# Keeping eleven instead of ten of sixteen key tiles of an attention in SBUF, with the closing layer norm redistributed over the engines

## The chip, the core and the metric

The kernel runs on one core of one Trainium2 chip, as one program. The metric is the device time of one execution in microseconds (us). Before the change it is 3533.81 us, the median of three runs (3532.12 to 3534.32). An engine's name is short: PE is the matrix engine (TensorE), DVE the vector engine, ACT the scalar engine, POOL is GpSimd, SP the engine that issues the DMAs.

## The reference

Two layers act on `x` (2 batches, 2048 tokens, 512 features), both modulated by a vector `cond` for each batch. The first is a state-space block (S5) with a feed-forward part. The change touches nothing of it. The second is the attention:

```python
def _sln(h, w, ln_g, ln_b, Wg, bg, Wb, bb):
    mu = jnp.mean(h, axis=-1, keepdims=True)
    var = jnp.mean((h - mu) ** 2, axis=-1, keepdims=True)
    ln = (h - mu) / jnp.sqrt(var + EPS) * ln_g + ln_b
    return (w @ Wg.T + bg)[:, None, :] * ln + (w @ Wb.T + bb)[:, None, :]
...
    h = _sln(hidden, w, ln_g, ln_b, Wg, bg, Wb, bb)
    qkv = (h @ Wqkv.T + bqkv).reshape(B, N, num_heads, hd, 3)
...
    energy = jnp.einsum('bhqd,bhkd->bhqk', q, k)
    att = jax.nn.softmax(energy, axis=-1) / D ** 0.5
    out = jnp.einsum('bhqk,bhkd->bhqd', att, v)
...
    out = out @ Wp.T + bp
    h1 = out + hidden
    h2 = _sln(h1, w, ln_g, ln_b, Wg, bg, Wb, bb)
    return h2 + h1
```

There are 16 heads of 32 features. The softmax goes over 2048 keys, and its maximum is taken exactly, for each query.

## The kernel before

**Up to about 1400 us** the S5 and feed-forward layers run. They leave `x2` (the residual), the keys `kd`, the queries `qd` and the values `vd` in DRAM.

**The attention** fills the rest. It is cut into 64 *blocks*: one block is one pair of heads against one chunk of 512 queries of one batch. Batch 0 has blocks 0 to 31, batch 1 (called `LB`) blocks 32 to 63. A block has 16 key tiles of 128 keys. It is worked in 8 *periods* of 2 key tiles. Periods are numbered through by `j`. `j % 8` is called the *phase* here: phase 0 is the first period of a block. The loop over `j` writes the order of every engine by hand; nothing reorders it.

For a key tile, the scores `s` (128 keys by 2 heads by 512 queries) are made on PE in PSUM (`raw_scores`, two banks, double-buffered). To subtract the maximum before the exponential, the maximum over all keys must be known first. The kernel does this in two ways:

- `NX` = 10 tiles of a block are *kept*. `AHEAD` = 15 periods before their use, `keep` makes their scores, ACT copies them into a tile of the `ring` (21 SBUF tiles, L766), and DVE folds them into a running maximum `run` (L771; the first tile of a block, tile 0, needs no fold of its own).
- The other 6 are made twice: first, ahead, in `across` with queries and keys exchanged (`m`, 384 key columns for each of 2 products, L780), from which DVE takes a maximum along the row (L785); and again at their use in `make` (L755), where DVE adds the negative maximum while it moves them out of PSUM (L820).

`turn_run` transposes the running maximum (PE, four 128x128, twice a block) and reduces it on DVE (L792). `spread` transposes the result (`pt_neg`, L802), has ACT copy it, and sends it through DRAM back to all partitions as `shift`. `take_off` adds `shift` to a kept tile on POOL (L814), in place. `exponentials` is ACT (L825). `weighted` multiplies by the values one period later (PE, 8 instructions, L835).

So a period is, in the order of PE: anything due, then either one `make` and `across` and one `keep`, or `across` and two `keep`s, and last the eight `o` products. Two `keep`s at once stand in phases 0 and 4. In those phases both tiles that are used are kept ones, so no `make` is needed. `twice` = (3, 7) names these periods counted in the block that is read ahead.

PSUM has 8 banks: `s` two times two, `m` two, one called `pt` and one for `o`. `m` and `pt` have one buffer each. `pt` is shared by the transposes of `turn_run` and `spread`, by the output projection `py` of batch 0 and by `z` of the closing norm. Two instructions of different engines that read the same bank are put in order by semaphores: the fold of a kept tile on DVE waits until ACT has copied it.

**The output** of a batch is finished per row tile of 128 queries: `fetch` loads, `divide` divides by the softmax sums (POOL), `project` multiplies by `wp` (PE, 8 instructions of 512 columns, L906), `residual`, `statistics`, `newton` (reciprocal square root, on ACT as one chain of 128x1 instructions), `last_norm` (ACT, into `z` in PSUM), `gain` (DVE), `close` (POOL and the store). For batch 0 its 16 row tiles run beside blocks 34 to 59, two for every three blocks, with one group of `project` in a period. For batch 1 twelve row tiles run from block 60 on, one every two periods. The last four are finished by `end_last`, after the last block. `after(j, ...)` puts work at the start of period `j`, `closing(j, ...)` behind that period's keeps and exponentials.

Of the kernel before, what the change touches and what calls it, by code (L numbers as in the profile page):

```python
# [19 lines left out]
P = 128  # L20
# [19 lines left out]
def tile_s5_block_then_sln_attention(  # L40
# [49 lines left out]
    one_half = const.tile([P, 1], F32, name="one_half")  # L90
    nc.gpsimd.memset(one_half, 1.5)
# [609 lines left out]
    NX = 10  # L701
# [4 lines left out]
    ring = ctx.enter_context(tc.tile_pool(name="ring", bufs=21, side="right"))  # L706
# [169 lines left out]
    def fetch(b, qt):  # L876

        at = slice(qt * P, (qt + 1) * P)
        o4 = work.tile([P, NG, P], F32, name="o4")
        nc.sync.dma_start(o4, od[b][:, at].rearrange("(g r) q -> r g q", r=P))  # L880
        by = work.tile([P, NG, P], F32, name="by")
        heads = invd[b][:, at].rearrange("(g j) q -> j g q", j=4)
        for j in range(4):
            nc.sync.dma_start(
                by[32 * j : 32 * j + 32, :, :], heads[j : j + 1, :, :].to_broadcast([32, NG, P])
            )
        xr = work.tile([P, D], F32, name="xr", bufs=4)
        nc.sync.dma_start(xr, x2[b][at, :])
        held[b, qt] = o4, by, xr
# [19 lines left out]
    def residual(b, qt):  # L909

        o4, h, py = held[b, qt]
        nc.vector.tensor_add(h, py, h)
        held[b, qt] = h

    def statistics(b, qt):

        h = held[b, qt]
        st = small.tile([P, 6], F32, name="st3")
        nc.vector.bn_stats(st, h)
        mv = small.tile([P, 2], F32, name="mv3")  # L920
        nc.vector.bn_aggr(mv, st)
        v = small.tile([P, 1], F32, name="v3")
        y = small.tile([P, 1], F32, name="scale3", bufs=4)
        shift = small.tile([P, 1], F32, name="shift3", bufs=4)
# [5 lines left out]
        nc.vector.tensor_scalar(shift, mv[:, 0:1], -1.0, None, ALU.mult)  # L930
        held[b, qt] = h, y, shift, v

    def newton(b, qt, turns, final):

        h, y, shift, v = held[b, qt]
        for _ in range(turns):
            c = small.tile([P, 1], F32, name="c3")
            nc.scalar.activation(c, y, AF.Identity, scale=y)
            nc.scalar.activation(c, c, AF.Identity, bias=one_half, scale=v)
            nc.scalar.activation(y, c, AF.Identity, scale=y)  # L940
        if final:
            nc.scalar.activation(shift, shift, AF.Identity, scale=y)

    def last_norm(b, qt):

        h, scale, shift, _ = held[b, qt]
        z = ps.tile([P, CH], F32, name="z", tag="pt")
        nc.scalar.activation(z, h, AF.Identity, bias=shift, scale=scale)
        held[b, qt] = h, z

    def gain(b, qt):

        h, z = held[b, qt]
        nc.vector.tensor_tensor(z, z, ending[b][0], ALU.mult)
        nc.vector.tensor_tensor(h, z, h, ALU.add)

    def close(b, qt):

        h, z = held.pop((b, qt))
        nc.gpsimd.tensor_tensor(h, h, ending[b][1], ALU.add)  # L960
        nc.sync.dma_start(out[b, qt * P : (qt + 1) * P, :], h)
# [9 lines left out]
    def end_fetch():  # L971
# [12 lines left out]
        late = P - 2 * HD  # L984
        nc.gpsimd.memset(ends["o"][1][late:, 1, :], 0.0)
        nc.gpsimd.memset(ends["w"], 0.0)
        nc.gpsimd.tensor_copy(ends["turn"], ident)
        for e in range(2):
            to, of = 3 * HD * e, HD + HD * e
            nc.sync.dma_start(ends["w"][to : to + HD, :], wp[late + HD * e : late + HD * e + HD, NG - 1, :])  # L990
            nc.gpsimd.tensor_copy(ends["turn"][:, to : to + HD], ident[:, of : of + HD])

    def end_fetch_more():
        cols = slice(LC * CH, (LC + 1) * CH)
        nc.sync.dma_start(ends["o"][1][: P // 2, 1, :], od[LB][D - P : D - P // 2, cols])

    def end_divisors(heads):
        cols = slice(LC * CH, (LC + 1) * CH)
        for j in heads:
            at = slice(HD * (j % 4), HD * (j % 4) + HD)  # L1000
# [4 lines left out]
    def end_divide(g, rows=P):  # L1005
        o, by = ends["o"][g // 2][:rows, g % 2, :], ends["by"][g // 2][:rows, g % 2, :]
        nc.gpsimd.tensor_tensor(o, o, by, ALU.mult)
# [19 lines left out]
    def end_last(o):  # L1027
        raw, inv, on = (spare(n)[:, 0, :] for n in ("raw4", "inv4", "on4"))
# [7 lines left out]
        for i, at in enumerate(parts):  # L1036
            nc.vector.reciprocal(inv[:, at], turned[:, i, :])
            nc.vector.tensor_tensor(on[:, at], o[:, at], inv[:, at], ALU.mult)
        end_project(1, list(range(NG - 1)))
        for i in range(2):  # L1040
            end_project(i, [NG - 1])
        mv = small.tile([P, TT, 2], F32, name="mv4")
        hts = [spare("ht01"), spare("ht23")]
        g_row, t_row = ending[LB]
        for i in range(2):
# [8 lines left out]
            nc.scalar.copy(hts[i], ends["py", i])  # L1054
        v = small.tile([P, TT], F32, name="v4")
        scale = small.tile([P, TT], F32, name="scale4")
        shift = small.tile([P, TT], F32, name="shift4")
        nc.vector.tensor_scalar(v, mv[:, :, 1], EPS, None, ALU.add)
        rsqrt(v, scale, TT)
        nc.vector.scalar_tensor_tensor(shift, mv[:, :, 0], -1.0, scale, ALU.mult, ALU.mult)  # L1060
        for t in range(TT):
            z = ends["py", t // 2][:, t % 2, :]
            nc.scalar.activation(
                z, z, AF.Identity, bias=shift[:, t : t + 1], scale=scale[:, t : t + 1]
            )
        for t in range(TT):
            qt = LC * TT + t
            y, z = hts[t // 2][:, t % 2, :], ends["py", t // 2][:, t % 2, :]
            nc.vector.tensor_tensor(z, z, g_row, ALU.mult)
            nc.vector.tensor_tensor(y, z, y, ALU.add)  # L1070
            (nc.gpsimd if t < TT - 1 else nc.vector).tensor_tensor(y, y, t_row, ALU.add)
            nc.sync.dma_start(out[LB, qt * P : (qt + 1) * P, :], y)
# [5 lines left out]
    AHEAD = 15  # L1078
    NP = 8
    twice = (3, 7)  # L1080
# [28 lines left out]
    SPREAD = -3  # L1109
    OPEN = -4  # L1110
    for i, n in enumerate(opens):
        free = NP * (max(m for m in range(N) if pair_of[m] == i - 2) + 1) if i > 1 else FIRST
        after(max(free if i > 1 else FIRST, NP * n - AHEAD - 11), load_k, i)
        after(max(OPEN + 2, NP * n - 9), load_v, i)
    for n in range(N):
        after(max(FIRST + 1 + n, NP * n - AHEAD - 6), load_q, n)
        after(NP * n - AHEAD + NP + 1, turn_run, n, 0)
        after(NP * n - AHEAD + NP + 3, turn_run, n, 1)
        after(NP * n + SPREAD, spread, n)
    for b in range(NB):  # L1120
        for c in range(NQ):
            j = NP * (blocks.index((b, NPAIR - 1, c)) + 1) + 1
            if (b, c) == (LB, LC):
# [8 lines left out]
                after(j + 5, end_divisors, range(NH - 4, NH - 2))  # L1132
                for g in range(NG - 1):
                    after(j + 3 + g, end_divide, g)
                after(j + 8, end_divide, NG - 1, P // 2)
# [8 lines left out]
            for t in range(TT):  # L1144
                qt = c * TT + t
                if b == LB:
# [6 lines left out]
                    closing(k + 3, newton, b, qt, 2, False)  # L1153
                    closing(k + 4, newton, b, qt, 1, True)
                    closing(k + 4, last_norm, b, qt)

                    (after if (k + 5 - SPREAD) % NP == 0 else closing)(k + 5, gain, b, qt)
                    closing(k + 6, close, b, qt)
                else:

                    k = NP * (NPAIR * NQ * (b + 1) + 2 + 3 * qt // 2) + 3
                    after(k - 2, fetch, b, qt)
                    after(k + 2, divide, b, qt)
                    for g in range(NG):
                        after(k + 3 + g, project, b, qt, (g,))
                    closing(k + 6, residual, b, qt)
                    closing(k + 7, statistics, b, qt)
                    for i in range(3):
                        closing(k + 8 + i, newton, b, qt, 1, i == 2)

                    k += 2 if t % 2 else 8
                    closing(k + 10, last_norm, b, qt)
                    closing(k + 11, gain, b, qt)
                    after(k + 13, close, b, qt)
# [120 lines left out]
```

## Time and profile before

The profiled execution took 3533.44 us; its span in the trace is 3531.7 us, with 34142 instructions.

| | PE | DVE | ACT | POOL |
|---|---|---|---|---|
| busy, us | 3378.7 | 2204.6 | 1976.7 | 1943.5 |
| share of the span | 96% | 62% | 56% | 55% |

The start times of the 64 `pt_neg` transposes, one for each block, three periods before it begins, give the length of a block:

| blocks | what runs beside | length of one block, us |
|---|---|---|
| 2 to 33 | nothing | 28.8 |
| 35 to 58 | norm and projection of batch 0 | 32.6, 33.2, 32.3 in turn |
| 61, 62 | norm and projection of batch 1 | 51.7, 52.7 |
| from the last `pt_neg` to the end | the last five periods, `end_last` | 96.0 |

How it is read: a busy PE counts a matmul from issue to its modelled end, so pipelined matmuls overlap, and busy PE time isn't PE at its peak. Start-to-start distances are what it sustains. The granted clock of PE is full nearly everywhere; six short stretches after 1400 us are at half clock, where PE had just stood idle.

### The profile page before, as it was taken

The page shows a single profiled execution, that of the slowest core. Times are in us where ns is not written, and L with a number is a line of the kernel's source. Part 1 is how long each engine was busy: PE and PEld are TensorE (multiplying, and loading weights), DVE is VectorE, ACT ScalarE, POOL GpSimd, SP SyncE. Part 2 cuts the span into 40 slices and gives each one's busy share as a digit, 9 for nine tenths or more (in the row PEclk, how much of TensorE's full clock was granted, in tenths as well). Part 3 has the DMA queues.
Part 4 walks back from the last instruction along what each step waited for, and adds up shares of the span by engine and source line. Part 5 has one row for each costly group of instructions (what it writes and reads, how often), then busy time and mean ns, then how long its engine had stood idle before and what let it go on. Part 6 is the DMA issues. An engine that isn't in the chain of part 4 may idle for free.

```text
span 3531.7 us, 34142 instructions
## 1 busy us (share of the span) xinstructions
PE 3378.7 (96%) x11772; PEld 1534.2 (43%) x11772; DVE 2204.6 (62%) x2937; ACT 1976.7 (56%) x2430; POOL 1943.5 (55%) x982
## 2 busy tenths in 40 slices
PE   7999999999999999899999999999999999999977
PEld 4444444444444444444444444444444444444432
DVE  6233232323232212689999999998888888888864
ACT  2111111111111111488888888888888888888865
POOL 4223131313131311288877888888687787777764
PEclk8999999999999999999999999999999999999999
DMA  8001111111111012332213222222233333323222
GB/s 298 1 30 42 48 39 45 39 50 37 48 36 42 33 45 74 99 71 65 71 50 73 71 65 65 53 72 66 68 85 84 81 76 79 88 71 80 61 89 93
DMA packets 201542, 236.92 MB, mean 67 GB/s; under 512 B 89755, under 2 KB 118939, under 8 KB 197273
## 3 DMA queue, kind: packets, MB, share of 16 engines
q1 hardware_dynamic: 201368, 234.74, 23.9%
q8 instruction: 93, 1.52, 0.2%
q14 instruction: 81, 0.66, 0.1%
HBM read 166.77 MB, written 67.76 MB: 66 GB/s over the span
## 4 chain that ended last, share of the span: by engine, by line
PE 71%; DVE 14%; ACT 11%; issue 2%; DMA 1%; POOL 1%; SPq 0%; DVEq 0%; ACTq 0%; POOLq 0%
PE o L835 14%; PE ph L489 13%; PE po L502 12%; PE s L755 9%; DVE run L771 8%; PE pk L532 6%; ACT x L766 4%; PE pv L544 3%; PE py L906 3%; ACT x L825 3%; PE m L780 2%; ACT pT L825 2%; DVE pT L820 2%; PE pt_run L791 2%; PE pu L423 2%
## 5 line engine op out<-in xcount | busy, mean ns | idle before, releaser
L814 POOL TENSOR_TENSOR x<-x,shift 128x1024 f32<-128x1024 f32 x640 | 1502.7, 2388 | 343.4 <-DMA shift<-flat 269.4
L766 ACT COPY x<-s 128x1024 f32<-128x1024 f32 x640 | 633.7, 1011 | 234.0 <-PE s L755 232.3
L755 PE MATMUL s<-qs,ks 128*128 128x512 f32 x2048 | 703.1, 433 | 51.7 <-DVE run L771 46.8
L825 ACT ACTIVATE x<-x 128x1024 f32<-128x1024 f32 x640 | 675.9, 1057 | 6.7 <-POOL x L814 6.6
L771 DVE TENSOR_TENSOR run<-s,run 128x1024 f32<-128x1024 f32 x512 | 625.4, 1221 | 82.1 <-ACT x L766 64.4
L835 PE MATMUL o<-x,v 128*64 128x512 f32 x2560 | 664.2, 614 | 2.0 <-ACT raw L844 2.0
L820 DVE TENSOR_TENSOR pT<-s,shift 128x1024 f32<-128x1024 f32 x384 | 467.6, 1218 | 55.0 <-PE s L755 50.4
L785 DVE TENSOR_REDUCE top<-m 128x1 f32<-128x768 f32 x512 | 485.8, 949 | 25.7 <-PE m L780 25.4
L755 PEld LDWEIGHTS s<-qs,ks 128*128 128x128 f32 x2048 | 344.9, 189 | 312.2 <-DVE run L771 143.3
L489 PE MATMUL ph<-fT,w_sb 128*128 128x512 f32 x1024 | 462.5, 596 | 0.0
L502 PE MATMUL po<-w_sb,hid 128*128 128x512 f32 x1024 | 460.3, 592 | 0.0
L825 ACT ACTIVATE pT<-pT 128x1024 f32<-128x1024 f32 x384 | 407.0, 1060 | 50.2 <-DVE pT L820 50.2
L493 ACT ACTIVATE hid<-ph,vec 128x512 f32<-128x512 f32 x128 | 87.9, 687 | 595.1 <-PE ph L489 595.1
L835 PE MATMUL o<-pT,v 128*64 128x512 f32 x1536 | 395.2, 593 | 3.8 <-ACT pT L825 3.8
L160 DVE SCALAR_TENSOR_TENSOR lo<-pk,vec,hi 128x512 fp32r<-128x512 f32 x64 | 48.1, 751 | 503.3 <-ACT hi L159 497.4
L780 PE MATMUL m<-ks,qs 128*128 128x384 f32 x1024 | 285.8, 360 | 16.3 <-DVE top L785 14.4
L489 PEld LDWEIGHTS ph<-fT,w_sb 128*128 128x128 f32 x1024 | 193.0, 192 | 228.2 <-issue 228.2
L502 PEld LDWEIGHTS po<-w_sb,hid 128*128 128x128 f32 x1024 | 190.7, 190 | 221.5 <-issue 221.5
L159 ACT ACTIVATE hi<-pk,vec 128x512 fp32r<-128x512 f32 x64 | 44.0, 687 | 393.3 <-PE pk L532 388.8
L436 POOL TENSOR_TENSOR m<-m,m 128x512 f32<-128x512 f32 x8 | 13.1, 1643 | 448.9 <-DVE m L434 448.9
L835 PEld LDWEIGHTS o<-x,v 128*64 128x64 f32 x2560 | 138.5, 135 | 260.7 <-issue 146.3
L512 POOL TENSOR_TENSOR x<-x,gated 128x512 f32<-128x512 f32 x32 | 39.6, 1268 | 354.3 <-DVE gated L511 354.3
(252 smaller groups left out, 2857.9 us busy)
## 6 DMA issues: line engine op xcount, KB each, us to landing
ks<-kd SPq DMA_DIRECT2D x128, 256.0 KB
qs<-qd SPq DMA_DIRECT2D x512, 64.0 KB
shift<-flat SPq DMA_DIRECT2D x64, 512.0 KB
x<-in_x SPq DMA_DIRECT2D x8, 1024.0 KB
w_sb<-in_w SPq DMA_DIRECT2D x8, 1024.0 KB
x<-x SPq DMA_DIRECT2D x8, 1024.0 KB
kd<-hi SPq DMA_DIRECT2D x32, 256.0 KB
kd<-lo SPq DMA_DIRECT2D x32, 256.0 KB
```

The costliest lines, as they stand in the source:

```text
L489: nc.tensor.matmul(ph, w1_sb[:, k, f * P : (f + 1) * P], fts[b, c][:, k, :], start=k == 0, stop=k == KC - 1)
L502: nc.tensor.matmul(pos[b, c][:, t, :], hid[:, t * P : (t + 1) * P], w2_sb[:, f, :], start=f == 0, stop=f == FC - 1,)
L532: nc.tensor.matmul(pk, w[:, k, g * P : (g + 1) * P], hT[:, k, :], start=k == 0, stop=k == KC - 1)
L755: nc.tensor.matmul(s[:, e, :], kst[pair_of[n], e][:, kt * P : (kt + 1) * P], qst[n][:, e, :], start=True, stop=True,)
L766: nc.scalar.copy(x, s)
L771: nc.vector.tensor_tensor(runs[n], s, kept[n, 0] if kt == 1 else runs[n], ALU.max)
L780: nc.tensor.matmul(m[:, i, :YW], qst[n][:, e, t * P : (t + 1) * P], kst[pair_of[n], e][:, k : k + YW], start=True, stop=True,)
L785: nc.vector.tensor_reduce(tops[n][:, j, 0:1], m[:, :, :YW], AX.XY, ALU.max, negate=True)
L814: nc.gpsimd.tensor_tensor(x, x, shifts[n], ALU.add)
L820: nc.vector.tensor_tensor(x, s, shifts[n], ALU.add)
L825: nc.scalar.activation(x, x, AF.Exp)
L835: nc.tensor.matmul(outs[n][64 * e : 64 * e + 64, :], v[:, kt, e : e + 2, :], x[:, e, :], start=first, stop=final,)
```

## The change

One more tile is kept, so `across` has 5 tiles (320 columns in each product), `make` has 5 per block, and there are three phases with two keeps (0, 2 and 4). The ring has 22 tiles and the maxima run 14 periods ahead. The second half of `turn_run` follows the first in the next period (phases 3 and 4; before, 2 and 4). `spread` stays in phase 5.

The closing norm of batch 0 no longer goes through `z`: the sum of projection and residual stays in PSUM (`py`); DVE reads it twice in `gain`, once as (h - mean) * gain row and once as h + shift row; POOL works out the reciprocal root in `turns`; ACT scales; POOL adds in `close`. For batch 1 the reciprocal root goes to DVE (`deviation`), and the two additions to POOL. In `end_last` the last group of heads of all rows is one product instead of two, ACT's copies and its norm fall away, POOL does the reciprocal root while DVE prepares both terms.

```diff
-    NX = 10
+    NX = 11
-    ring = ctx.enter_context(tc.tile_pool(name="ring", bufs=21, side="right"))
+    ring = ctx.enter_context(tc.tile_pool(name="ring", bufs=22, side="right"))
-        xr = work.tile([P, D], F32, name="xr", bufs=4)
+        xr = work.tile([P, D], F32, name="xr", bufs=3)
...
     def residual(b, qt):
-        nc.vector.tensor_add(h, py, h)
+        o4, xr, py = held[b, qt]
+        if b == LB:
+            nc.vector.tensor_add(xr, py, xr)
+            held[b, qt] = xr, xr, None
+        else:
+            nc.vector.tensor_add(py, py, xr)
+            held[b, qt] = py, xr, o4.rearrange("p g q -> p (g q)")
...
-    def newton(b, qt, turns, final):
-        for _ in range(turns):
-            nc.scalar.activation(c, y, AF.Identity, scale=y)
-            nc.scalar.activation(c, c, AF.Identity, bias=one_half, scale=v)
-            nc.scalar.activation(y, c, AF.Identity, scale=y)
+    def newton(eng, y, v):
+        for _ in range(3):
+            c = small.tile([P, 1], F32, name="c3")
+            eng.tensor_scalar(c, y, y, v, ALU.mult, ALU.mult)
+            eng.tensor_scalar(y, c, 1.5, y, ALU.add, ALU.mult)
+    def turns(b, qt):
+        newton(nc.gpsimd, *held[b, qt][-2:])
+    def gain(b, qt):
+        nc.vector.scalar_tensor_tensor(w, h, mv[:, 0:1], ending[b][0], ALU.subtract, ALU.mult)
+        nc.vector.tensor_tensor(ht, h, ending[b][1], ALU.add)
+    def scaled(b, qt):
+        nc.scalar.activation(w, w, AF.Identity, scale=y)
+    def close(b, qt):
+        nc.gpsimd.tensor_tensor(ht, w, ht, ALU.add)
+        nc.sync.dma_start(out[b, qt * P : (qt + 1) * P, :], ht)
+    def deviation(b, qt):
+        newton(nc.vector, y, v)
+        nc.vector.tensor_scalar(shift, mv[:, 0:1], -1.0, y, ALU.mult, ALU.mult)
     def last_norm(b, qt):
         z = ps.tile([P, CH], F32, name="z", tag="pt")
         nc.scalar.activation(z, h, AF.Identity, bias=shift, scale=scale)
+        y = work.tile([P, D], F32, name="y", bufs=1)
+        nc.vector.tensor_tensor(y, z, ending[b][0], ALU.mult)
+    def last_close(b, qt):
+        nc.gpsimd.tensor_tensor(h, h, ending[b][1], ALU.add)
+        nc.gpsimd.tensor_tensor(y, y, h, ALU.add)
+        nc.sync.dma_start(out[b, qt * P : (qt + 1) * P, :], y)
...
     def end_last(o):
-            nc.vector.tensor_tensor(on[:, at], o[:, at], inv[:, at], ALU.mult)
+            for r in (slice(0, HD), slice(3 * HD, P)):
+                nc.vector.tensor_tensor(on[r, at], o[r, at], inv[r, at], ALU.mult)
         end_project(1, list(range(NG - 1)))
-        for i in range(2):
-            end_project(i, [NG - 1])
...
-            nc.scalar.copy(hts[i], ends["py", i])
-        rsqrt(v, scale, TT)
+        for _ in range(3):
+            nc.gpsimd.tensor_tensor(c, scale, scale, ALU.mult)
+            nc.gpsimd.tensor_tensor(c, c, v, ALU.mult)
+            nc.gpsimd.tensor_scalar(c, c, 1.5, None, ALU.add)
+            nc.gpsimd.tensor_tensor(scale, scale, c, ALU.mult)
+        for t in range(TT):
+            nc.vector.scalar_tensor_tensor(w, h, mv[:, t, 0:1], g_row, ALU.subtract, ALU.mult)
+            nc.vector.tensor_tensor(ht, h, t_row, ALU.add)
         for t in range(TT):
-            nc.vector.tensor_tensor(z, z, g_row, ALU.mult)
-            nc.vector.tensor_tensor(y, z, y, ALU.add)
-            (nc.gpsimd if t < TT - 1 else nc.vector).tensor_tensor(y, y, t_row, ALU.add)
+            nc.vector.scalar_tensor_tensor(ht, w, scale[:, t : t + 1], ht, ALU.mult, ALU.add)
...
-    AHEAD = 15
-    twice = (3, 7)
+    AHEAD = 14
+    twice = (0, 2, 6)
...
         after(NP * n - AHEAD + NP + 1, turn_run, n, 0)
-        after(NP * n - AHEAD + NP + 3, turn_run, n, 1)
-        after(NP * n + SPREAD, spread, n)
+        after(NP * n - AHEAD + NP + 2, turn_run, n, 1)
+        after(NP * n - AHEAD + NP + 3, spread, n)
...
-                    closing(k + 3, newton, b, qt, 2, False)
-                    closing(k + 4, newton, b, qt, 1, True)
-                    closing(k + 4, last_norm, b, qt)
-                    (after if (k + 5 - SPREAD) % NP == 0 else closing)(k + 5, gain, b, qt)
-                    closing(k + 6, close, b, qt)
+                    after(k + 4, deviation, b, qt)
+                    after(k + 5, last_norm, b, qt)
+                    after(k + 6, last_close, b, qt)
                 else:
-                    k = NP * (NPAIR * NQ * (b + 1) + 2 + 3 * qt // 2) + 3
-                    after(k - 2, fetch, b, qt)
-                    after(k + 2, divide, b, qt)
-                    for g in range(NG):
-                        after(k + 3 + g, project, b, qt, (g,))
-                    closing(k + 6, residual, b, qt)
-                    closing(k + 7, statistics, b, qt)
-                    for i in range(3):
-                        closing(k + 8 + i, newton, b, qt, 1, i == 2)
-                    k += 2 if t % 2 else 8
-                    closing(k + 10, last_norm, b, qt)
-                    closing(k + 11, gain, b, qt)
-                    after(k + 13, close, b, qt)
+                    k = NP * (NPAIR * NQ * (b + 1) + 2 + 3 * qt // 2)
+                    after(k, fetch, b, qt)
+                    after(k + 3, divide, b, qt)
+                    for g in range(3):
+                        closing(k + 5 + g, project, b, qt, (g,))
+                    after(k + 8, project, b, qt, (3,))
+                    closing(k + 8, residual, b, qt)
+                    closing(k + 8, statistics, b, qt)
+                    closing(k + 9, gain, b, qt)
+                    after(k + 11, turns, b, qt)
+                    closing(k + 12, scaled, b, qt)
+                    after(k + 14, close, b, qt)
```

The rest of the diff moves rows and loads of `end_fetch`, so that the divided part of the last group and the late heads lie in one tile (`ends["o"][1]`, with the rows of `wp` permuted to match).

## The prediction

> **What bounds the kernel now.** I read the page's busy table first: PE is at 96%, so the question is what PE waits for in each stretch. The costliest groups give the prices, and the stretches between stages the room on each engine.
>
> ```profile
> L814 POOL TENSOR_TENSOR x<-x,shift 128x1024 f32<-128x1024 f32 x640 | 1502.7, 2388 | 343.4 <-DMA shift<-flat 269.4
> L766 ACT COPY x<-s 128x1024 f32<-128x1024 f32 x640 | 633.7, 1011 | 234.0 <-PE s L755 232.3
> L771 DVE TENSOR_TENSOR run<-s,run 128x1024 f32<-128x1024 f32 x512 | 625.4, 1221 | 82.1 <-ACT x L766 64.4
> L820 DVE TENSOR_TENSOR pT<-s,shift 128x1024 f32<-128x1024 f32 x384 | 467.6, 1218 | 55.0 <-PE s L755 50.4
> L785 DVE TENSOR_REDUCE top<-m 128x1 f32<-128x768 f32 x512 | 485.8, 949 | 25.7 <-PE m L780 25.4
> ```
>
> POOL is idle 343 us in the attention, 269 of them until `shift` has landed; nobody waits for POOL there. The table by stretches (plain blocks; norm of batch 0; norm of batch 1; from the last `pt_neg` on):
>
> ```profile
> core 0: us, PE busy (x) PEld busy (x) DVE busy (x) ACT busy (x) POOL busy (x), PEclk, DMA share, GB/s
> 1533.10:2454.50 921.40, 904.80 (x3874) 411.13 (x3872) 839.18 (x837) 822.51 (x897) 752.24 (x322) 1.00 0.27 65
> 2486.70:3271.10 784.40, 746.13 (x3035) 329.99 (x3033) 678.66 (x769) 673.48 (x849) 601.06 (x272) 1.00 0.32 78
> 3271.10:3435.70 164.60, 140.23 (x541) 61.29 (x540) 122.49 (x163) 126.70 (x187) 113.29 (x57) 0.97 0.27 77
> 3435.70:3531.70 96.00, 71.77 (x207) 27.22 (x207) 43.63 (x89) 47.11 (x87) 47.02 (x32) 0.89 0.29 91
> ```
>
> Plain blocks are nearly full on PE, with DVE and ACT at 91% and 89%; in the other stretches PE stands idle more. Where it stops in a plain block is seen in the timeline of a two-keep phase (start, duration, then in brackets the idle time before and its releaser):
>
> ```profile
> 2206.50 1.08 PE L755 MATMUL s<-qs,ks 128*128 128x512 f32 x4
> 2207.16 1.93 ACT L766 COPY x<-s 128x1024 f32<-128x1024 f32 x2
> 2208.21 2.55 DVE L771 TENSOR_TENSOR run<-s,run 128x1024 f32<-128x1024 f32 x2 [0.55 <-ACT x L766]
> 2210.81 0.72 PE L755 MATMUL s<-qs,ks 128*128 128x512 f32 x2 [0.24 <-DVE run L771]
> ```
>
> Two score tiles are made; each must be copied (ACT), then folded (DVE), before the next period's second score tile has a bank. This row of copies and folds is serial, and PE waits at its end. The waits name the same place, once after each two-keep phase (64 times in 32 blocks):
>
> ```profile
> PE s L755 <- DVE run L771: 15.6, 64, 0.3
> POOL x L814 <- DMA shift<-flat: 115.5, 22, 6.9
> POOL x L814 <- DVE pT L820: 36.1, 7, 5.7
> POOL x L814 <- DVE top L785: 17.6, 3, 6.2
> ```
>
> From the `o` products I read eight period lengths of a plain block, from phase 1 to the next phase 0: 3.96, 3.74, 3.37, 3.74, 3.96, 3.35, 3.34, 3.35, sum 28.8 us. The two 3.96 follow the two-keep phases, the two 3.74 hold `turn_run` (four transposes at 109 ns).
>
> **Plain blocks (2 to 33 and 59, some 33).** `across` loses 64 of 384 columns in 16 products a block. *The rule:* the Trainium skill, "TensorE: Matmul & The Clock Gate", section "Back-to-back issue gap", gives an isolated gap of N/2.4 + 2.5 ns, so 26.7 ns for 64 columns, but says that a sustained stream takes only 81 ns at N = 128 and 131 ns at N = 512; that would be 8 ns for 64 columns, 0.13 us a block. *The row:* in this trace's stream the distance from start to start is 109 ns at 128 columns, 176 at 384 and 235 at 512. It doesn't agree with the sustained figures, and its slopes (0.26 and 0.46 ns per column) give 17 to 30 ns. I take 26 ns: 16 x 26 = 0.42 us a block, against 0.13 by the sustained rule.
>
> But a period pinned by copies and folds keeps nothing of it. I write the new block as a schedule, from the start of phase 0:
> - Phases 0, 1: two keeps in phase 0, as before. End 7.30 (3.35 + 3.96), no gain.
> - Phase 2: new tiles 0 and 1. Tile 0 starts `run` without a fold. Tile 1's fold waits for the second copy, which in phase 0 ends 3.05 after the start: 10.35. From there DVE is full. Start-to-start distances of before's rows: fold 1.28; phase 3 `top` of `turn_run` 0.61, `pT` 1.13, `m` reduction 0.73 (0.86 less 128 elements at 1.05 ns, the slope between a 512-element row at 0.69 and a 1024-element row at 1.22), fold 1.28; phase 4 `top` 0.72, `neg` 0.09, reduction 0.73, two folds 1.33 and 1.22. Sum 9.12, so 19.47. Phase 5's second score tile then starts at 19.5, and 2.53 later phase 5 ends (as in the timeline): 22.05. Before: 7.31 + 3.74 + 3.37 + 3.74 + 3.96 = 22.12.
> - Phases 6, 7: 3.28 each, 6.56 instead of 6.69.
>
> The block is 28.6, 0.2 less; DVE distances can be 0.1 off in ten instructions, so I allow 28.4 to 29.0, the upper end being a third stall of full size: (3.96 - 3.35 = 0.61) - 0.42 = +0.2. I take -0.25 x 33 = **-8 us** (-13 to +7).
>
> What this loads elsewhere, per block: ACT one copy (1.01) more, 25.7 to 26.7 of 28.5; DVE one fold more, one `pT` less, 8 x 0.13 off the reductions, 26.2 to 25.2; POOL one take-off more. SP's queue issues the same loads, at the same distance from their use; the ring's 22 tiles are just enough, as a `keep` takes the tile whose last `o` product stands right ahead of it on PE. Nothing of these three ends last unless their cover is gone (the rivals).
>
> *The rule against this change:* "GPSIMD Engine Reference", section "4.1 Engine selection", says elementwise work belongs on the vector engine, GpSimd taking about twice as long for two inputs. The rows agree on the price: 2388 ns against 1218. By the rule 64 adds moved to POOL cost 64 x 1.17 = +75 us. By the waits above they cost nothing: POOL stood idle 115.5 + 36.1 + 17.6 = 169 us in 32 blocks, 5.3 a block, and 2.33 (start to start) fit, leaving 2.9. I take nothing, since the smallest lead of a take-off before its exponential is about 1.9 to 2.8 us now, and some 1.4 then by the same schedule.
>
> **Norm of batch 0 (8 times three blocks with two row tiles each).** The triple now takes 98.06 us, 11.7 over three plain blocks. `project` explains 2 x 8 x 0.43 = 6.9; the rest, 4.8, is 2.4 us of stall in each row tile: ACT's nine 128x1 turns and its norm, DVE's residual, statistics and gain, and the hold on `pt`:
>
> ```profile
> L939 ACT ACTIVATE c<-c,one_half,v 128x1 f32<-128x1 f32 x48 | 18.6, 387 | 1.6
> L938 ACT ACTIVATE c<-scale 128x1 f32<-128x1 f32 x48 | 13.5, 282 | 0.0
> ```
>
> ACT loses the nine (3 x (0.28 + 0.39 + 0.30) = 2.9 us) and shift's one, keeps one scaling of 512. DVE's five 512-element operations (0.69 each) become five with the same sources, but now in two periods instead of five, about 2.1 us of residual and statistics and 1.4 of gain. They stand in phases 0, 1, 4 or 5, where a fold waits behind them; so not the whole stall goes. I take 1.4 of the 2.4, so 3.44 + 1.4 a row tile, over blocks of 28.5: 3 x 28.5 + 2 x 4.84 = 95.2; -2.9 x 8 = **-23 us** (-42: no stall left; 0: all given back to DVE). POOL's six small operations aren't in the trace: between 0.1 us each (its smallest, a 128x1 memset) and 1.0; nearest is a 128x8 copy at 0.19, so 1.2 us a row tile, in POOL's idle time.
>
> **Norm of batch 1 (blocks 60 to 63).** Here PE waits for `pt`, which `z` holds until `gain` and its waiting transposes stall PE to half clock:
>
> ```profile
> PE pt_run L791 <- DVE xr L955: 10.2, 4, 3.5
> PE pt_neg L802 <- DVE xr L955: 7.7, 2, 4.7
> 3383.00 0.37 PE L802 MATMUL pt_neg<-ident,neg 128*8 128x128 f32 x1 [3.04 <-DVE xr L955]
> 3383.16 4.92 PE L906 MATMUL py<-wp,o 128*128 128x512 f32 x8
> ```
>
> The eight `py` took 4.92, at full clock 3.44. After, `z` is filled and read at the start of one period, before the transposes are due again, and the turns lie on DVE (7 x 0.19 = 1.3 us), beside `project`'s 3.44. An undisturbed pair of periods takes 7.42 + 4.34 = 11.76, four of them 47.0; blocks 61 and 62 take 51.7 and 52.7. I take their excess, 10.4, and 5 for the same waits behind them: **-15 us** (-22: waits 17.9 and half of the slow stretches; -3: DVE's turns hold the next fold instead). The wait that is new, `y` for its store (one buffer), lies two periods after it.
>
> **Tail.** 8 of 20 products of 0.43 go: -3.4. ACT's copies and norm leave the chain; POOL's 13 small operations (13 x 0.26 = 3.4) run beside eight DVE operations (8 x 0.7 = 5.6), then 4 x 0.7 end it: about -1.5. **-5 us** (-2 to -7). The lead-in (14 instead of 15 periods ahead, more keeps in it) I put at 0, +-3.
>
> **Sum:** -8 - 23 - 15 - 5 = -51 on the profiled 3533.4 (span 3531.7 and 1.7 around it): 3482.4; the median shown lies 0.4 above: **3483**.
>
> **Rivals.**
> 1. *The third two-keep phase stalls in full* (wait of `s` for `run` takes the gain's place). For it: DVE is full from 10.35 to 19.5 in my schedule. Against: tile 0 has no fold. Plain +0.2 x 33 = +7, norm stage (-2.9 + 3 x 0.45 = -1.5) x 8 = -12, the others -12 and -5: -22, **3512**.
> 2. *Slower: POOL ends last.* Eleven take-offs at 2.33 are 25.6 of 28.5; in the norm stage 33 x 2.33 + 2 x (divide and close, as now, + 1.2) comes to 89%. Place: the last take-offs of a block, ahead of ACT's exponential and so of `o`. If `shift` or a take-off comes x later than in my schedule, each of 57 blocks loses x - 1.4; it is slower than before from x = 2.4 (57 x 1.0 = 57 against 51). For it: `shift`'s waits vary up to 6.9 us. At x = 2.9: +85 - 51 = +34, **3568**. Against: the shift arrives 5.6 to 7.2 us after `pt_neg`, its phase isn't moved, and many waits end on DVE, not on the transfer.
> 3. *The norm stages give more than I took* (-35, -22, -7, and -13 in the plain blocks): 3457. A part of the likeliest.
>
> **How the numbers follow.** Likeliest 0.66, own range 3458 to 3502; rival 1 0.2 (3502 to 3526); rival 2 0.1; no change between 0.04. A measurement tells 0.2%, 7 us, from no change. The range 3455 to 3522 leaves out rival 2, a part of rival 1 and the gains over rival 3. Faster 0.86, same 0.04, slower 0.10.
>
> **What would show it.** Plain blocks of 28.4 to 28.6 with `s` waiting for `run` in phases 1 and 5 and not 3; triples near 95; POOL's wait for `shift` at about 2.9 a block, and next to no waiting of ACT's exponentials for POOL; no wait of some us for `pt` after 3271; the tail 5 shorter. Wrong would be: ACT waiting for take-offs, a stall in phase 3, or triples above 97.

## The result, and the profile after

The changed kernel takes 3496.13 us (median of four runs, 3492.06 to 3497.32) beside 3532.97 us; the ratio is 0.9893, with a 95% interval of 0.9876 to 0.9911. The forecast was 3483 us: the direction and the range (3455 to 3522) held, but of the 51 us that were summed up only 37 came.

The profiled execution has a span of 3495.3 us (time 3497.08). Cut at the same `pt_neg` transposes as in the prediction, the difference lies here:

| stretch, us | before | after | difference | forecast |
|---|---|---|---|---|
| start to `pt_neg` of block 2 (lead-in) | 1533.1 | 1537.1 | +4.0 | 0 |
| plain blocks 2 to 33 | 921.4 | 913.5 | -7.9 | -8 |
| norm of batch 0, blocks 34 to 58 | 816.5 | 805.7 | -10.8 | -23 |
| blocks 59 to 62 | 164.6 | 148.3 | -16.3 | -15 |
| from the last `pt_neg` on | 96.0 | 90.8 | -5.2 | -5 |

Three of five terms fit to about a microsecond (block 59 is a plain block, counted with the plain ones in the forecast; for blocks 59 to 62 the fit is partly luck, see below). The norm stage gave half, and the lead-in lost 4.

The groups that were shown of before, on the page of the profile after:

```profile
L812 POOL TENSOR_TENSOR x<-x,shift 128x1024 f32<-128x1024 f32 x704 | 1654.1, 2390 | 159.9 <-DMA shift<-flat 135.8
L764 ACT COPY x<-s 128x1024 f32<-128x1024 f32 x704 | 692.4, 1012 | 212.8 <-PE s L753 211.6
L769 DVE TENSOR_TENSOR run<-s,run 128x1024 f32<-128x1024 f32 x576 | 703.0, 1220 | 82.0 <-ACT x L764 59.0
L783 DVE TENSOR_REDUCE top<-m 128x1 f32<-128x640 f32 x512 | 417.7, 816 | 40.7 <-PE m L778 38.1
L818 DVE TENSOR_TENSOR pT<-s,shift 128x1024 f32<-128x1024 f32 x320 | 389.5, 1217 | 57.6 <-PE s L753 57.6
```

64 more take-offs, copies and folds, 64 fewer `pT`; no duration has changed except the reduction, 949 to 816 ns (the prediction's slope gave 815). POOL's idle time ahead of its take-offs fell from 343 to 160 us. The windows of the same stretches (plain, norm of batch 0, norm of batch 1, the end; the second row begins at block 34 here, at block 35 in the prediction):

```profile
core 0: us, PE busy (x) PEld busy (x) DVE busy (x) ACT busy (x) POOL busy (x), PEclk, DMA share, GB/s
1537.10:2450.60 913.50, 891.88 (x3875) 399.11 (x3873) 807.77 (x837) 848.50 (x929) 825.13 (x353) 1.00 0.27 66
2450.60:3256.20 805.60, 763.37 (x3171) 337.62 (x3169) 681.43 (x779) 675.33 (x744) 714.05 (x404) 0.99 0.34 79
3256.20:3404.50 148.30, 137.37 (x542) 58.95 (x540) 124.19 (x198) 107.44 (x120) 128.70 (x65) 1.00 0.27 80
3404.50:3495.30 90.80, 64.98 (x199) 24.40 (x197) 48.85 (x111) 28.27 (x33) 59.09 (x50) 0.91 0.35 107
```

In plain blocks ACT has 93% and POOL 90%, and still PE sets the time (98%). In the norm stage PE's busy share is lower (95%, as before), and its clock is no longer full (0.99): something stops it there. The clock in the norm of batch 1 went from 0.97 to 1.00.

The two-keep phase in a plain block, and the waits of the plain blocks:

```profile
2232.57 1.09 PE L753 MATMUL s<-qs,ks 128*128 128x512 f32 x4
2233.28 1.91 ACT L764 COPY x<-s 128x1024 f32<-128x1024 f32 x2
2234.32 2.55 DVE L769 TENSOR_TENSOR run<-s,run 128x1024 f32<-128x1024 f32 x2 [0.72 <-ACT x L764]
2236.93 0.50 PE L753 MATMUL s<-qs,ks 128*128 128x512 f32 x1 [0.30 <-DVE run L769]
```

```profile
POOL x L812 <- DMA shift<-flat: 69.7, 26, 5.4
PE s L753 <- DVE run L769: 19.5, 64, 0.3
POOL x L812 <- DVE pT L818: 11.4, 4, 3.6
POOL x L812 <- DVE top L783: 7.2, 2, 3.7
ACT x L823 <- POOL x L812: 0.8, 2, 0.4
```

The row of copies and folds is as long as before. PE waits for `run` still 64 times in 32 blocks, not 96: the third two-keep phase has added no wait of this kind. POOL's three rows add up to 88 us, 2.8 a block (forecast 2.9), and ACT's exponentials wait for POOL for 0.8 us in all: POOL does not end last.

Where the norm stage stops is in its waits and in the timeline of a block in which a row tile is finished (from phase 0 to phase 2):

```profile
PE m L778 <- DVE top L783: 21.0, 15, 1.4
```

```profile
2690.94 0.82 DVE L783 TENSOR_REDUCE top<-m 128x1 f32<-128x640 f32 x1 [1.74 <-PE m L778]
...
2694.92 0.69 DVE L914 TENSOR_TENSOR py<-py,xr 128x512 f32<-128x512 f32 x1
2695.64 0.70 DVE L921 BATCH_NORM_STATS2 st<-py 128x6 f32<-128x512 f32 x1
...
2697.06 1.23 DVE L818 TENSOR_TENSOR pT<-s,shift 128x1024 f32<-128x1024 f32 x1
...
2698.20 0.81 DVE L783 TENSOR_REDUCE top<-m 128x1 f32<-128x640 f32 x1
...
2699.07 0.56 PE L778 MATMUL m<-ks,qs 128*128 128x320 f32 x2 [1.41 <-DMA qs<-qd]
```

At the start of phase 0 DVE is idle for 1.74 us. Residual and statistics take it from 2694.92 to 2697.06; only then come phase 1's `pT` and the reduction of its `m`. `m` has one buffer, so phase 2's product starts at 2699.07, 1.41 us late. (Its bracket names a DMA. But 15 of 16 such waits are put down to `top`, and here too the reduction ends only 0.06 us before; the DMA was most likely just the last event of this wait.)

### The profile page after: what moved, and what is told of

Same layout as the page of the kernel before. It is cut to its first block, busy times and chain, and to the rows that moved or that the text cites. A ratio compares the mean times of both kernels' runs of the same rounds, so it can differ in the third digit from the quotient of the medians.

```text
span 3495.3 us, 34359 instructions
## 1 busy us (share of the span) xinstructions
PE 3343.7 (96%) x11764; PEld 1509.3 (43%) x11764; DVE 2153.1 (62%) x2976; ACT 1942.2 (56%) x2208; POOL 2137.7 (61%) x1162
## 4 chain that ended last, share of the span: by engine, by line
PE 73%; DVE 13%; ACT 8%; DMA 2%; issue 2%; POOL 2%; SPq 0%; DVEq 0%; ACTq 0%; POOLq 0%
PE o L833 15%; PE ph L487 13%; PE po L500 13%; PE s L753 10%; DVE run L769 9%; PE pk L530 6%; ACT x L764 4%; PE pv L542 3%; PE py L904 3%; PE m L778 3%; PE pt_run L789 2%; PE pu L421 2%; ACT x L823 1%; ACT pT L823 1%; PE pt_tf L149 1%
## 5 line engine op out<-in xcount | busy, mean ns | idle before, releaser
L812 POOL TENSOR_TENSOR x<-x,shift 128x1024 f32<-128x1024 f32 x704 | 1654.1, 2390 | 159.9 <-DMA shift<-flat 135.8
L764 ACT COPY x<-s 128x1024 f32<-128x1024 f32 x704 | 692.4, 1012 | 212.8 <-PE s L753 211.6
L769 DVE TENSOR_TENSOR run<-s,run 128x1024 f32<-128x1024 f32 x576 | 703.0, 1220 | 82.0 <-ACT x L764 59.0
L823 ACT ACTIVATE x<-x 128x1024 f32<-128x1024 f32 x704 | 739.6, 1060 | 14.7 <-POOL x L812 14.5
L833 PE MATMUL o<-x,v 128*64 128x512 f32 x2816 | 720.4, 613 | 0.0
L783 DVE TENSOR_REDUCE top<-m 128x1 f32<-128x640 f32 x512 | 417.7, 816 | 40.7 <-PE m L778 38.1
L818 DVE TENSOR_TENSOR pT<-s,shift 128x1024 f32<-128x1024 f32 x320 | 389.5, 1217 | 57.6 <-PE s L753 57.6
L823 ACT ACTIVATE pT<-pT 128x1024 f32<-128x1024 f32 x320 | 339.4, 1060 | 67.3 <-DVE pT L818 67.3
L833 PE MATMUL o<-pT,v 128*64 128x512 f32 x1280 | 333.5, 600 | 13.4 <-ACT pT L823 13.4
L778 PE MATMUL m<-ks,qs 128*128 128x320 f32 x1024 | 261.5, 337 | 29.1 <-DVE top L783 25.7
## 6 DMA issues: line engine op xcount, KB each, us to landing
ks<-kd SPq DMA_DIRECT2D x128, 256.0 KB
kd<-hi SPq DMA_DIRECT2D x32, 256.0 KB
kd<-lo SPq DMA_DIRECT2D x32, 256.0 KB
```

What stands on the lines that cost most here:

```text
L764: nc.scalar.copy(x, s)
L769: nc.vector.tensor_tensor(runs[n], s, kept[n, 0] if kt == 1 else runs[n], ALU.max)
L778: nc.tensor.matmul(m[:, i, :YW], qst[n][:, e, t * P : (t + 1) * P], kst[pair_of[n], e][:, k : k + YW], start=True, stop=True,)
L783: nc.vector.tensor_reduce(tops[n][:, j, 0:1], m[:, :, :YW], AX.XY, ALU.max, negate=True)
L812: nc.gpsimd.tensor_tensor(x, x, shifts[n], ALU.add)
L818: nc.vector.tensor_tensor(x, s, shifts[n], ALU.add)
```

## The experiments

Times stand beside the kernel before of the same chip (3532.7, 3532.3 or 3532.5 us) and beside the changed kernel's 3496.1.

**1. The tiles without the norm.** Only NX, the ring, AHEAD, `twice` and the places of `turn_run` change (and, in batch 1, the old `gain` stands at the start of phase 3, ahead of `turn_run`, where else it would stand behind it):

```diff
-    NX = 10
+    NX = 11
-    AHEAD = 15
-    twice = (3, 7)
+    AHEAD = 14
+    twice = (0, 2, 6)
```

> The kernel before with only the key-tile part of the change (eleven kept tiles, 22 ring tiles, three two-keep phases, maxima 14 periods ahead); norm and tail as before. By the schedule of the prediction: plain blocks 28.5 as in the whole change, so -8 us there, about -0.3 a block in the 24 norm blocks (-7), +4 for the lead-in seen in the changed kernel's trace: about 3522 us. Rival (the third two-keep phase stalls as soon as DVE also carries the old norm): norm triples at 98 or more, the sum near 3530. Rival (most of the whole gain is from the tiles): below 3510.

Measured: 3549.0 us, ratio 1.0047 (1.0032 to 1.0062). **Slower than before.** Plain blocks give the same -7.9, but the old norm takes 822.4 instead of 816.5, and blocks 59 to 62 take 178.6 instead of 164.6. In its window from 3330 to 3450 us, the waits of PE for the bank `pt`, which `z` holds, have grown to

```profile
PE pt_neg L802 <- DVE xr L955: 12.4, 2, 6.4
PE pt_run L791 <- DVE xr L955: 12.2, 2, 6.4
```

PE's mean granted clock in blocks 59 to 62 is 0.93, before it was 0.97. None of the three expectations reached this high. In batch 1 `z` is held from the end of an even phase into the odd one after it, and phase 3 now has transposes, where before only phase 5 had. That this is the reason is likely; it wasn't tried apart.

**2. The norm without the tiles.** NX, ring, AHEAD, `twice` and `turn_run` of before; all else of the change.

> The changed kernel with ten kept tiles and the old 15 periods of lead; only the new norm and tail remain of the change. Theory: plain blocks 28.8; norm triples 86.4 + 2 x (3.44 + 1.8) = 96.9 instead of 98.06 (-9); batch 1's norm -16, tail -5; no loss in the lead-in: about 3503 us. Rival (the new norm needs the second reading of py at a place only the new phases leave free): triples at 98 or above, about 3513.

Measured: 3536.9 us, ratio 1.0014 (1.0004 to 1.0024), with a wide spread over 12 runs (3523 to 3544). Blocks 59 to 62 give -15.5 and the end -3.9, as in the whole change; the norm of batch 0 **loses** 22.8. The rival's mechanism was right, its size far too small. Waits from 2600 to 3200 us, and the place:

```profile
PE pt_run L789 <- DVE xr L947: 33.8, 12, 3.1
```

```profile
3018.63 0.68 DVE L947 TENSOR_TENSOR xr<-py,t_row 128x512 f32<-128x512 f32 x1
3019.37 0.66 PE L789 MATMUL pt_run<-ident,run 128*128 128x128 f32 x4 [2.79 <-DVE xr L947]
```

`py` lies in `pt` until `gain` has read it, late in phase 1. Here `turn_run` stands at phase 2, and PE waits 2.8 us for the bank. The stage also has nine stretches at half clock (below).

**9. One line of the tiles' part added to experiment 2.**

```diff
-        after(NP * n - AHEAD + NP + 1, turn_run, n, 0)
+        after(NP * n - AHEAD + NP + 2, turn_run, n, 0)
```

> The kernel with ten tiles and the new norm (3536.9 us), with one difference: the two halves of turn_run stand in phases 3 and 4, as in the whole change, instead of 2 and 4. Theory (the new norm keeps py in the pt bank until gain, in phase 1, and turn_run in phase 2 waits for it 2.8 us, so it was the phase of turn_run and not the eleventh tile that the norm needed): the norm triples fall from 99 to 103 us to 97, the stage from 839 to about 813, the whole to about 3510 us. Rival (the narrower across or the third two-keep phase opens the room): the stage stays above 830, the whole above 3527.

Measured: 3501.7 us, ratio 0.9911 (0.9896 to 0.9926), 8 us better than the theory. The norm stage falls from 839.3 to 803.3, and no `pt_run` wait is left in it. So in the whole change the phases of `turn_run` were worth 35 us to the new norm, and the eleventh tile itself 5.6 (3501.7 - 3496.1; 4.7 more went to the longer lead-in, 1537.1 beside 1532.4).

**3. Statistics at the start of phase 0.**

```diff
-                    after(k + 8, project, b, qt, (3,))
-                    closing(k + 8, residual, b, qt)
-                    closing(k + 8, statistics, b, qt)
+                    closing(k + 7, project, b, qt, (3,))
+                    after(k + 8, residual, b, qt)
+                    after(k + 8, statistics, b, qt)
```

> The changed kernel; the fourth group of project closes phase 7 instead of opening phase 0, and residual and statistics of batch 0 stand at the start of phase 0 instead of its end; gain stays. Theory: in the changed kernel residual and statistics hold DVE for 2.1 us ahead of phase 1's pT, so its m reduction is late and PE waits 1.4 us for m in phase 2, once in each row tile; at the start of phase 0 DVE idles 1.74 us anyway. The stall of 1.8 a row tile falls to about 0.5: 16 x 1.3 = -20 us, and the half-clock stretches behind that wait go too (-5): 3471 to 3478 us. Rival (it is the amount of DVE work, not its place): the wait moves to phase 1's s, time within 5 us of 3496.

Measured: 3462.5 us, ratio 0.9805 (0.9788 to 0.9821): 33.6 us below the changed kernel and below the expected range. The blocks with a row tile fall from 33.73 to 31.89: 28.5 and the 3.44 of `project`, nothing more. 16 x 1.84 = 29 us, and the three half-clock stretches go too. Of the waits of PE for other engines from 2600 to 3200 us this one is left:

```profile
PE s L753 <- DVE run L769: 12.7, 41, 0.6
```

It was the place of this DVE work, not its amount: the stage's DVE busy time is 678 us here and 681 there. (The fourth group of `project` had to move with it, from the start of phase 0 to the end of phase 7; the two moves weren't tried apart. That the waits of `m` for `top` are gone speaks for DVE's work.)

**7. PE's columns alone taken back.** 384 columns again, of which the reduction reads 320.

```diff
-                m[:, i, :YW], ..., kst[pair_of[n], e][:, k : k + YW],
+                m[:, i, : YW + 64], ..., kst[pair_of[n], e][:, k - 64 : k + YW],
```

> The changed kernel with 384 columns again in each product of across (the 64 extra are of a kept tile, and the reduction still reads 320). It takes back PE's saving alone. Theory (26 ns a product, of which a pinned period keeps nothing): the free phases 6, 7 and one more lose 0.05 each, block 28.51 to about 28.65, +8 us over 57 blocks. Rival (all columns count): 0.42 a block, +24 us. Rival (8 ns a product, as in a sustained stream): phases 6 and 7 lose under 0.02 each, +1 to +3 us.

Measured: 3511.0 us, ratio 0.9941 (0.9926 to 0.9956), 14.9 above the changed kernel, between the theory (+8) and the first rival (+24). Plain blocks take 28.81 instead of 28.52, which is before's 28.79: **the whole gain of the eleventh tile in a plain block is the 64 columns**; the third two-keep phase, net of DVE's shorter reductions (kept here), costs 0.02. Its periods from phase 1 on are 3.96, 3.34, 3.73, 3.73, 4.02, 3.33, 3.33, 3.35 us (block 12), those of the changed kernel 3.99, 3.29, 3.68, 3.69, 4.01, 3.28, 3.29, 3.28. Six periods lose about 0.05 each, those of phases 2 to 4 among them; phases 1 and 5, which end in the wait of `s` for `run`, lose nothing. 0.29 us over 16 products are 18 ns for 64 columns, and over the twelve products of the six periods that lose, 24 ns: near the 26 taken, and well above the 8 ns that the sustained figures of the prediction's rule would make.

**10 and 11. The worth of the tile when no stall is left.** Experiment 3's edit and 4's in both (the pieces of the scaling in phase 7, not at the start of a block), with ten tiles (and 9's line) and with eleven.

> The kernel of e9 with residual and statistics at the start of phase 0 and the projection weights scaled in four pieces at the end of a block, where POOL waits for shift. Against e11, which is the same with eleven tiles, it gives the worth of the eleventh tile when no stall is left. Theory (0.29 us a block, all of it from the narrower across): e11 + 17 us, about 3472. Rival (with ten tiles DVE carries the norm less well, as its reductions are longer): above 3480.

> The changed kernel with the edits of e3 (early residual and statistics) and of e4, the four pieces of the scaling now at the start of phase 7 of blocks 2 to 5, where POOL has 2.6 us of waiting for shift. Theory: e3's 3462.5 less 7 for block 1, and nothing back in the plain blocks: 3455 us. Rival (the two overlap): 3460.

Measured: 3470.3 us (ratio 0.9822, 0.9806 to 0.9839) and 3454.2 us (0.9777, 0.9763 to 0.9792). The tile is worth 16.2 us. The second is the lowest of all, 78 us below before and 42 below the changed kernel; both expectations held within 2 us.

**4. The scaling of the projection weights.** In block 1 POOL scales them (5.37 us) between two take-offs. Chain and timeline of the changed kernel:

```profile
1513.18 5.37 POOL wp L1222
```

```profile
1521.03 1.06 ACT L823 ACTIVATE x<-x 128x1024 f32<-128x1024 f32 x1 [4.51 <-POOL x L812]
...
1524.30 1.22 PE L753 MATMUL s<-qs,ks 128*128 128x512 f32 x2 [3.94 <-DVE run L769]
```

```diff
-        if j == NP:
-            nc.gpsimd.tensor_scalar(wp, wp, ISQ, None, ALU.mult)
+        if j in (3 * NP, 4 * NP, 5 * NP, 6 * NP):
+            g = j // NP - 3
+            nc.gpsimd.tensor_scalar(wp[:, g, :], wp[:, g, :], ISQ, None, ALU.mult)
```

> The changed kernel; POOL's scaling of the projection weights (128x2048, 5.37 us, standing between the take-offs of block 1) is done in four pieces of 512 at the start of blocks 3 to 6 instead. Theory (rival 2 of the prediction, seen in one block): POOL is 5.37 late there, block 1 takes 35.6 instead of 28.5; it falls to about 28.6, and the pieces of 1.34 each cost less than 1 together: -5 to -7 us, about 3490. Rival (the long block 1 is a DMA or the lead-in's tail, not POOL): no change.

Measured: 3488.9 us, ratio 0.9878 (0.9863 to 0.9893), 7.2 below the changed kernel. Block 1 takes 28.51 instead of 35.64; the plain blocks give 1.7 back, nearly all of it in block 5 (30.23), and that goes too in experiment 11, where the pieces stand in phase 7.

**5 and 6. The cover of POOL.** Behind the first take-off of blocks 3 to 32 stands an operation of 1.34 or 2.68 us that changes nothing (`nc.gpsimd.tensor_scalar(wp[:, :1, :], wp[:, :1, :], 1.0, None, ALU.mult)`, or `:2`).

> The changed kernel with 1.34 us more on POOL in each of blocks 3 to 32: an in-place multiplication of 512 projection weights by 1.0, right behind the first take-off. Measures the cover of POOL. Theory (prediction's rival 2: a lead of about 1.4 us): nearly nothing, 0 to +8 us. Rival (the lead that counts is the smallest one of each block, 0.5 to 2 us, and each lateness comes back in every block): up to +20.

> The same with 2.68 us a block (1024 weights). Theory (price (x - 1.4) a block): (2.7 - 1.4) x 30 = +39 us, 3535. Rival (what counts is the idle time of POOL, 2.76 us a block, which 2.68 still fits): 0 to +5 us.

Measured, one time each: 3496.9 and 3519.8 us; the second lies between its theory (+39) and its rival (0 to +5). In the traces blocks 2 to 33 take 915.9 and 937.0 us instead of 913.5: 0.08 and 0.78 us for each of the 30 blocks in the mean. But with 1.34 us most blocks lose nothing; block 5 loses 1.4 and block 17 0.6. With 2.68 us block 5 loses 2.9 and the others 0.2 to 1.5. So the cover is 2.68 - 0.78 = 1.9 us in the mean, if all lateness beyond it is paid; by block, in this trace, it lies between 1.2 and 2.5, and block 5 has none. The waits of ACT's exponentials for take-offs grow from 0.8 us to 5.9 and 40.6. The idle time of 2.8 us, which would still have fitted 2.68, isn't what counts.

**8. `z` held for a period again, in batch 1 alone.**

```diff
-                    after(k + 5, last_norm, b, qt)
+                    closing(k + 4, last_norm, b, qt)
+                    if (k + 5) % NP == 3:
+                        due.setdefault(k + 5, []).insert(0, (last_gain, (b, qt)))
+                    else:
+                        (after if (k + 5) % NP == 5 else closing)(k + 5, last_gain, b, qt)
```

`last_gain` is the half of `last_norm` that reads `z`.

> The changed kernel; in the norm of batch 1 alone z is written behind the keeps of one period and read behind those of the next, as before, so that it holds the pt bank for about a period (in phase 3 it is read at the start, ahead of turn_run). The turns stay on DVE. Theory (the hold of pt made most of the waits): pt waits of 5 to 10 us come back, +6 to +12 us. Rival (taking the turns off ACT made the gain): within 3 us of the changed kernel.

Measured: 3516.4 us, ratio 0.9956 (0.9939 to 0.9973), 20.3 above the changed kernel, more than the +6 to +12 expected. Blocks 59 to 62 take 168.7 instead of 148.3, more than before's 164.6, with the turns still on DVE. From 3298 to 3418 us:

```profile
PE pt_run L789 <- DVE y L977: 7.0, 2, 4.6
PE pt_neg L800 <- DVE y L977: 6.2, 2, 3.9
```

In the changed kernel no such wait is left there. The rest is the clock: in this stretch of 120 us PE's mean granted clock is 0.93, in the changed kernel's (3284 to 3404 us) 1.00, which is some 8 us (an estimate: 0.07 x 120). The hold of the bank alone is thus enough to explain the term. What the move of the turns adds wasn't tried apart.

**12. The buffer of `y`.** In the last blocks of the changed kernel (3284 to 3500 us) DVE waits for the store of `y`, which has one buffer, and PE behind it:

```profile
DVE y L973 <- DMA out<-y: 14.9, 2, 10.9
PE o L833 <- ACT pT L823: 13.4, 5, 8.7
```

```diff
-        nc.gpsimd.tensor_tensor(y, y, h, ALU.add)
-        nc.sync.dma_start(out[b, qt * P : (qt + 1) * P, :], y)
+        nc.gpsimd.tensor_tensor(h, y, h, ALU.add)
+        nc.sync.dma_start(out[b, qt * P : (qt + 1) * P, :], h)
```

> The kernel of e11; in the norm of batch 1 POOL's last addition writes into the tile of h and the store goes from there, so that y (one buffer) is free once POOL has read it and not only when its store has landed. Theory (in the trace of the changed kernel DVE waits 14.9 us in two pieces for the store of y, and PE's o products 13.4 us behind it): -6 to -12 us against e11, 3443 to 3449. Rival (the wait moves to SP's queue, as the fetch three row tiles on needs the same tile): within 3 us of e11 or slower.

Measured: 3457.3 us, ratio 0.9783 (0.9769 to 0.9798); experiment 11 has 3454.2 and an interval that overlaps. No gain, so the rival held. The waits of PE from 3365 us on:

```profile
PE py L904 <- POOL o L891: 6.3, 2, 5.4
PE o L833 <- ACT pT L823: 5.1, 4, 1.4
```

The wait of `o` fell from 11.8 in experiment 11 to 5.1, and one of `project` for `divide` took its place (0.9 to 6.3), so the sum is 11.4 here, 12.7 there. The chain there goes back over `by` to loads queued on SP.

## Why the prediction was right, and where its sum was off

- **Plain blocks, -8: right (-7.9), with one wrong step inside.** The schedule of DVE is in the trace: tile 1's fold starts 10.35 us after phase 0 (2242.53 - 2232.18), and the folds of phase 4 end at 19.35 (forecast 19.47):

```profile
2242.53 1.23 DVE L769 TENSOR_TENSOR run<-s,x 128x1024 f32<-128x1024 f32 x1 [1.66 <-ACT x L764]
2248.98 2.55 DVE L769 TENSOR_TENSOR run<-s,run 128x1024 f32<-128x1024 f32 x2
```

  But a full DVE doesn't pin PE in phases 2 to 4. I let the columns count in phases 6 and 7 alone; by experiment 7 they count in six of eight periods, about 0.05 in each. "A pinned period keeps nothing of it" holds only for phases 1 and 5, which end in PE's wait. What I took as a small gain in DVE's row was the columns, and the sizes happened to be near (0.25 a block taken, 7.9 / 32 = 0.25 measured).
- **Norm of batch 0, -23: the mis-sized term (-10.8).** I took 1.4 us of stall a row tile; it is 33.73 - 28.52 - 3.44 = 1.8. The triple is 96.0, not 95.2, which makes 6 us over eight. Most of the other 6 are three stretches at half clock (blocks 36, 44 and 53 are 1.7 to 2.1 longer), of which the sum had none. The mechanism, DVE's work in phases 0 and 1, was named, with the wrong one behind it: not "a fold waits behind them" but `m`, by its single buffer. The lower end of -42 was mis-added: no stall at all gives 98.06 - (3 x 28.5 + 2 x 3.44) = 5.7 a triple, -45, and experiment 3 reached it (771.8 beside 816.5, -44.7).
- **The norm was summed as if it stood alone.** It gains only with `turn_run` moved out of phase 2 (experiments 2 and 9). The sum held since both parts were in the change, but the step of moving `turn_run` was priced at nothing where it decides 35 us.
- **Norm of batch 1, -15: right (-16.3)**, by the mechanism given (experiment 8), but its two parts are wrong and offset each other. Blocks 61 and 62 fell from 51.7 and 52.7 to 42.8 and 44.5, by 17.1 and not 10.4: the 47.0 taken as undisturbed was too long. And the 5 for waits behind them isn't seen: from the last `pt_neg` to the end of the last block's `o` products it takes 65.9 us before and 66.3 after. That the sum fits is luck. "The wait that is new ... lies two periods after it" was wrong: DVE waits up to 10.9 us for the store. Taking it away gained nothing (experiment 12): the chain there ends on loads queued on SP instead.
- **Tail, -5: right (-5.2).** The twelve remaining products of 0.43 stand in the chain where twenty stood (the first line is of before):

```profile
3504.34 8.58 PE py L1022 x20
3473.63 5.15 PE py L1043 x12
3478.78 1.73 PE py L1067 x4
```

- **Lead-in, 0 +- 3: missed by one (+4.0).** 2.7 of it are block 1, where POOL's scaling stands (experiment 4). With the scaling there, block 1 takes 34.1 to 36.0 us in the traces with eleven tiles and 33.0 to 33.4 in those with ten; that the one take-off more is the reason is likely, not shown. The rest changes between builds (the first `pt_neg` starts between 1468.6 and 1473.2 us in the traces) and stays open.
- **Rival 1 fell**: the third two-keep phase costs 0.02. **Rival 2's** point was set too early: its 1.4 us of cover measured 1.9 in the mean. Its price, lateness less cover in every block, is the assumption behind that figure and isn't shown apart; one cover for all blocks is too simple, as block 5 has none. POOL's turns take 0.34 and 0.27 us, not 0.19, and were hidden all the same in the time of experiment 3.
- **The rule on GpSimd** would have made +75 us. Experiments 5 and 6 show from where on POOL's work costs time: about 1.9 us more in a block, in the mean.

## What to carry to other kernels

A bank or buffer that two jobs share has to be followed through all phases: the same norm lost 23 us or gained 13 with one transposition placed a period earlier or later, and the tiles alone made the kernel slower. Small vector work goes where its engine idles in the period: the same operations cost 1.8 us a row tile at the end of phase 0, ahead of work that PE waits for, and nothing at its start, where DVE was idle. The cover of a side engine is its smallest lead over the consumer, to be measured block by block, by adding work to it, and not its idle time.

## What the runs showed of the hardware that was not expected

PE's clock falls to half after a window that it didn't fill, and the windows run on their own beat. Around one stretch of the changed kernel (same columns as the windows above):

```profile
2793.54:2796.95 3.41, 1.91 (x10) 0.98 (x10) 3.41 (x5) 2.64 (x3) 2.91 (x8) 1.00 0.54 137
2796.95:2800.36 3.41, 3.41 (x8) 0.65 (x8) 2.40 (x3) 3.08 (x4) 3.41 (x2) 0.50 0.03 11
2800.36:2803.77 3.41, 3.41 (x20) 1.84 (x18) 2.65 (x4) 1.37 (x2) 3.41 (x3) 1.00 0.00 0
```

PE was idle for 1.5 of 3.41 us, and the next 3.41 us ran at half clock, with 8 matmuls for 20. The three stretches of the norm stage begin at 2540.94, 2796.94 and 3087.07 us: 256.0 and 290.1 us apart, 75 and 85 times 3.413. The Trainium skill, "TensorE: Matmul & The Clock Gate", section "What's actually happening", gives such a free-running window of 3413 ns, which agrees. It speaks of an idle window, and here the window was more than half busy. Laid on that beat, in the traces of the changed kernel and experiments 2, 6 and 7, all windows of the norm stage that ran at full clock with over 2.05 us of PE idle are followed by half clock and none with under 1.47; between them both occur. (One stretch of experiment 2 lasts two windows; the first of them, at half clock itself, was idle for 0.71.) So a wait of 1.4 us in each row tile costs 1.4 us mostly, and now and then 1.7 to 2.1 more, by where it falls on the beat. The number of such stretches likely also makes the spread of experiment 2's times. Only one of its runs has a trace, but every run's mean granted clock is on record: 0.989 in the fastest (3523.4 us), 0.983 or 0.984 in the four above 3542. The difference of about 0.0055 is some 19 us of the clock (an estimate: 0.0055 x 3540), and the spread is 20.
